# A two-layer graph attention kernel: the preparation steps split into bank fills and bank readers, and the last pair's rows kept in SBUF

## The chip, the core and the metric

The kernel runs on one core of a Trainium2 chip, in one launch. The metric is device time in microseconds, from the start to the end of one execution; lower is better. Engines are named as the profile names them: PE (TensorE), PEld (its weight loads), ACT (ScalarE), DVE (VectorE), POOL (GpSimd) and SP (SyncE, which issues the DMAs here).

## The reference, cut to what matters

A graph of N = 4096 nodes with D = 256 features and a 4096 x 4096 adjacency matrix passes through two graph attention layers (H = 8 heads of O = 32), and then through a transformer block masked by the same adjacency. The change touches the graph layers only:

```python
Wh  = jnp.einsum('nd,hdo->hno', x, W)
src = jnp.einsum('hno,ho->hn', Wh, a[:, :O])
dst = jnp.einsum('hno,ho->hn', Wh, a[:, O:])
e = jax.nn.leaky_relu(src[:, :, None] + dst[:, None, :], 0.2)
e = jnp.where(adj[None, :, :] > 0, e, NEG_INF)
out = jnp.einsum('hnm,hmo->hno', softmax(e), Wh)      # one layer, twice:
h = elu(layer(x, W1, a1)) + x;  out = elu(layer(h, W2, a2)) + h
```

## The kernel before, in words

The softmax is never formed. The exponential of a leaky ReLU is one of two products of a term of the row and a term of the column, and which of the two holds depends on the sign of src + dst. So a layer is a sum over neighbours m of values scaled by column terms, once over all neighbours and once over those with a positive sum. The sign becomes a matrix of eight-bit weights (the comparison), the adjacency masks it, and PE multiplies.

**Groups.** The stage runs 256 groups, one after the other: 2 layers l, 4 blocks nb of 8 row tiles, 4 pairs p of heads, 8 groups g of G = 4 column tiles. A group is 8 tiles x 4 column tiles, 32 units of three matmuls (line 1401), with six PSUM banks `bank0` to `bank5` that stay open over the eight groups of a pair. Each group uses 64 weights of `t` (two per unit), so that group i begins at the matmul on `t` number 64 i of the timeline. Groups are numbered 0 to 255 here; layer 1 begins at 128.

**Side work.** What ACT, DVE and POOL do for other groups, and some PE work, is issued between the tiles of a group. Each step has a place between 0 and 1 in the list `side`; after tile n the steps whose place lies in it are issued, so PE, ACT and DVE each get a fixed order written out by hand. The side work of group i is:

- the comparison for group i+2 (`compare`, lines 1100 and 1102): four steps of two 128x1024 comparisons, one on ACT and one on DVE (in some steps both on ACT), and the mask on DVE (line 1115). It writes `t8`, which has three buffers;
- in layer 0 the clipping of adjacency rows (`mask_clip`, line 867, DVE) and their turning (`mask_turn`, four PE transposes of line 890 and an ACT copy, line 892): four units per group in groups 0 to 5, about one later;
- after a pair, its end on DVE and ACT (`pair_end`, lines 1143 to 1186), a few steps per group;
- in groups 0 to 5 (layer 0) and in 122 to 127, 131 and 132 (layer 1) the preparation of four node tiles.

**Preparation.** `preparation(l, q, ...)` takes rows q of the layer's input (`g_rows`, four tiles of 128 x 256). Two steps `features` transpose one half of the columns each into a PSUM bank (PE, line 981) and copy it to `g_ft` (ACT, line 984). Four steps `values(t)` multiply (PE, line 994) and read the bank: a copy of the terms and three exponentials on ACT (lines 1001, 1007, 1008), then a reduction and a product on DVE (lines 1009, 1020, and 1026 from SBUF). Steps `split(t)` cut the product into two halves (ACT line 1032 or DVE line 1034, then POOL line 1035). `term_rows` transposes the row terms (PE line 1040), copies them (ACT line 1044) and stores them. `turn_bank` gives these steps and the turning of masks a bank each, out of two in turn (`turn`, bufs=2): a fill waits until all readers of the bank of two fills ago are done. In layer 1 the product has two buffers (`g_prod`).

**Rows between the layers.** The end of a pair of layer 0 adds the residual into a tile `e_x` and stores 64 columns of a block of 8 tiles to DRAM (`step_out`, lines 1185 and 1186). Layer 1 loads its rows from there (`rows_ahead`, line 743). The last two preparations, q = 6 and 7, need the columns of the last pair of the last block, whose end runs in groups 128 and 129. They are loaded in groups 130 and 131.

## Time and profile before

| | us |
|---|---|
| median of 3 runs (lowest to highest) | 3252.28 (3251.95 to 3252.8) |
| the profiled execution | 3250.22 |
| its span, from the first to the last instruction | 3248.4 |
| PE, PEld, DVE, ACT, POOL busy in it | 3099.1, 2717.4, 2804.6, 2703.1, 1177.5 |
| the graph layers' groups in it | 40.3 to about 1652 |

Busy shares over the whole span mix stages with different limits. The graph layers take half of it, and there PE, ACT and DVE are all nearly always busy in a plain group. So the preparation groups have to be read by themselves, with windows that begin and end at group starts.

### The profile page before, as it was taken

What the parts mean: (1) busy time and instruction counts of PE and PEld (TensorE: products, weight loads), DVE (VectorE), ACT (ScalarE), POOL (GpSimd) and SP (SyncE); (2) the same over time, 40 slices, a digit from 0 to 9 for tenths busy, and PEclk for the clock granted to TensorE, in tenths of its full rate; (3) what the DMA queues carried; (4) which work ended last, traced back from release to release, by engine and by line L of the source; (5) the groups of instructions that cost most, each with busy time, mean ns of one, the idle gap of its engine ahead of it and who ended that gap; (6) DMA issues with size and microseconds to landing.
All of it is one profiled execution on the core that took longest, in us unless ns stands there. A gap on an engine that the chain in (4) does not pass through costs nothing.

```text
span 3248.4 us, 139142 instructions
## 1 busy us (share of the span) xinstructions
PE 3099.1 (95%) x64076; PEld 2717.4 (84%) x64076; DVE 2804.6 (86%) x3102; ACT 2703.1 (83%) x3305; POOL 1177.5 (36%) x536
## 2 busy tenths in 40 slices
PE   5899999999889999999988999999999999997999
PEld 4799999999779999999965888888888888885666
DVE  6899999988889999999966999999999999994121
ACT  5799999999679999999964888888888888884332
POOL 2300000000310000000002998999888998893110
PEclk8999999999999999999999999999999999998999
DMA  7666554420310213120145010101101010004200
GB/s 250 203 198 201 167 185 149 148 74 29 105 42 31 84 54 93 42 75 27 38 121 143 14 40 20 33 27 27 32 24 47 14 40 15 20 7 120 69 33 27
DMA packets 210306, 249.30 MB, mean 77 GB/s; under 512 B 87792, under 2 KB 131056, under 8 KB 209712
## 3 DMA queue, kind: packets, MB, share of 16 engines
q1 hardware_dynamic: 209712, 240.31, 24.1%
q8 instruction: 503, 8.24, 1.1%
q14 instruction: 91, 0.75, 0.1%
HBM read 197.80 MB, written 42.47 MB: 74 GB/s over the span
## 4 chain that ended last, share of the span: by engine, by line
PE 44%; ACT 4%; DVE 3%; DMA 2%; issue 1%; POOL 0%; SPq 0%; POOLq 0%; DVEq 0%; ACTq 0%
PE u_ps L1725 15%; PE u_av L1743 14%; PE u_dn L1743 8%; PE misc L1931 3%; ACT t L1100 2%; PE misc L1668 2%; PE misc L1915 1%; PE misc L1687 1%; DMA u_xres<-rows 1%; DVE t L1102 1%; DVE t L1115 1%; PE misc L1488 1%; ACT ln_square L1455 0%; POOL u_xres L1874 0%; PE misc L1879 0%
## 5 line engine op out<-in xcount | busy, mean ns | idle before, releaser
L1401 PE MATMUL bank<-vst,t 128*128 128x132 f16 x16384 | 1451.0, 220 | 32.0 <-DVE t L1115 31.5
L1816 POOL TENSOR_TENSOR u_both<-u_e 128x1024 f32<-128x1024 f32 x448 | 1052.5, 2391 | 934.0 <-DVE u_e L1734 931.7
L1401 PE MATMUL bank<-vst,mask 128*128 128x66 f16 (+1 forms) x10296 | 1345.3, 206 | 0.0
L1100 ACT ACTIVATE t<-s_b,g_terms 128x1024 int8<-128x1024 f32 x1231 | 1318.9, 1154 | 27.6 <-PE bank L1401 21.7
L1401 PEld LDWEIGHTS <-t 128*128 128x128 fp8e4 x16384 | 1183.5, 97 | 47.1 <-DVE t L1115 36.6
L1734 DVE SCALAR_TENSOR_TENSOR u_e<-u_mask,u_ps 128x1024 f32<-128x1024 uint8 x1024 | 1165.9, 1215 | 10.3 <-ACT u_ps L1732 6.9
L1732 ACT ACTIVATE u_ps<-u_ps 128x1024 f32<-128x1024 f32 x1024 | 1030.1, 1009 | 142.1 <-PE u_ps L1725 44.0
L1401 PEld LDWEIGHTS <-mask 128*128 128x128 fp8e4 x10296 | 903.5, 98 | 0.0
L1115 DVE SCALAR_TENSOR_TENSOR t<-mask,t 128x2048 int32<-128x2048 int32 x256 | 591.3, 2310 | 82.6 <-ACT t L1100 72.4
L1725 PE MATMUL u_ps<-u_q,u_k 128*32 128x512 f16 x8192 | 637.1, 383 | 11.9 <-DVE u_e L1734 11.2
L1743 PE MATMUL u_av<-u_e,u_v 128*32 128x128 f32 x16384 | 601.8, 273 | 0.6 <-issue 0.6
L1743 PEld LDWEIGHTS u_av<-u_e,u_v 128*32 128x32 f32 x16384 | 488.9, 110 | 129.5 <-issue 2.6
L1102 DVE TENSOR_SCALAR t<-s_b,g_terms 128x1024 fp8e4<-128x1024 f32 x817 | 583.8, 747 | 2.6 <-DMA s_b<-s_d 2.6
L1035 POOL TENSOR_TENSOR vst<-g_prod,vst 128x528 f16<-128x528 f32 x36 | 44.2, 1244 | 777.8 <-DVE vst L1034 757.4
L1743 PE MATMUL u_dn<-u_both,u_ones 128*32 128x128 f32 x7168 | 280.2, 273 | 0.0
L1725 PEld LDWEIGHTS <-u_k 128*32 128x32 f16 x8192 | 228.6, 95 | 57.4 <-issue 16.2
L1743 PEld LDWEIGHTS u_dn<-u_both,u_ones 128*32 128x32 f32 x7168 | 212.9, 110 | 41.1 <-issue 0.5
L1922 ACT ACTIVATE u_hid<-misc,n_b 128x512 f32<-128x512 f32 x64 | 42.7, 682 | 149.5 <-PE misc L1915 149.5
L1938 DVE TENSOR_TENSOR u_xres<-u_xres,misc 128x256 f32<-128x256 f32 x32 | 13.5, 421 | 121.1 <-PE misc L1931 121.1
L1931 PE MATMUL misc<-u_w,u_hid 128*128 128x256 f32 x512 | 111.8, 379 | 0.0
L1915 PE MATMUL misc<-ln_cols,u_w 128*128 128x512 f32 x256 | 111.2, 592 | 0.0
L1931 PEld LDWEIGHTS misc<-u_w,u_hid 128*128 128x128 f32 x512 | 96.8, 190 | 13.2 <-issue 0.5
(147 smaller groups left out, 1916.4 us busy)
## 6 DMA issues: line engine op xcount, KB each, us to landing
g_adj<-in_adj_dram SPq DMA_DIRECT2D x123, 512.0 KB
s_b<-s_d SPq DMA_DIRECT2D x64, 512.0 KB
mask<-mask SPq DMA_DIRECT2D x128, 256.0 KB
u_mask<-mask SPq DMA_DIRECT2D x32, 512.0 KB
mask<-stage SPq DMA_DIRECT2D x48, 256.0 KB
rows<-e_x SPq DMA_DIRECT2D x32, 256.0 KB
half_d<-u_halves SPq DMA_DIRECT2D x32, 256.0 KB
u_q<-half_d SPq DMA_DIRECT2D x32, 256.0 KB
```

Source lines behind the costliest of these rows:

```text
L1100: nc.scalar.activation(to.bitcast(I8), s, AF.Sign, bias=negd, scale=-1.0)
L1102: nc.vector.tensor_scalar(to, s, negd, -1.0, op0=ALU.is_ge, op1=ALU.mult, saturate=False)
L1115: nc.vector.scalar_tensor_tensor(both, m32.unsqueeze(1).to_broadcast(list(both.shape)), SIGNS, both, op0=ALU.bitwise_or, op1=ALU.bitwise_and,)
L1401: nc.tensor.matmul(to, left, right, start=k not in opened, stop=last)
L1668: nc.tensor.matmul(pq, wq_sb[k][:, i * D + c * P : i * D + (c + 1) * P], hn[:, k, :], start=(k == 0), stop=(k == DC - 1),)
L1725: nc.tensor.matmul(ps[r * O : (r + 1) * O, j, :], k_st[:, h, at : at + O], q_st[:, h, :], start=True, stop=True,)
L1732: nc.scalar.activation(ps, ps, AF.Exp, scale=SCALE)
L1734: nc.vector.scalar_tensor_tensor(e, mask, 0.0, ps, op0=ALU.not_equal, op1=ALU.mult)
L1743: nc.tensor.matmul(to[j * O : (j + 1) * O, at], lefts[j], es[j // 2][:, j % 2, at], start=first and part == 0, stop=last and part == PARTS ...
L1816: nc.gpsimd.tensor_tensor(both, es_of[i - 1][u], es_of[i][u], op=ALU.add)
L1915: nc.tensor.matmul(ph, w1_sb[:, k, f * P : (f + 1) * P], hn[:, k, :], start=(k == 0), stop=(k == DC - 1),)
L1931: nc.tensor.matmul(po[:, :D], hid[:, f, at : at + P], w2_sb[:, f, :], start=(f == 0), stop=(f == FC - 1),)
```

## The change

**Fill and readers apart.** Each bank's use in `preparation` and `mask_turn` becomes two steps: an "out" step that fills the bank on PE, and an "in" step that reads it. In the groups with preparation the uses stand in one list: two features, then each value behind a turn of a mask as long as there are any, then the term rows. This is eleven uses in layer 0, seven in layer 1. Use k is filled at place (k + 0.5) slots and read at (k + 0.5 + delay) slots; a slot is 0.9 / (number of uses) and delay is 0.3 with turns and 0.6 without. The split of a value comes 1.5 slots after its reading. The comparison's first place moves from 0.25 to 0.3 in these groups. In the value's reading the copy of the terms moves behind the three exponentials.

**Places by unit.** Side steps are issued after each unit of three matmuls, no longer after each tile, except that what is left waits for the end of the last tile.

**Rows inside SBUF.** For the last pair of layer 0's last block the residual sum is written by two DVE additions of four tiles straight into the `g_rows` tiles of q = 6 and 7, and stored from there with two DMAs. The other 192 columns of these tiles are loaded at the start of group 128. The loads in groups 130 and 131 are gone.

```diff
-        def features(c):
+        def features_out(c):
-            pt = bank()
+            pt = held["f", c] = bank()
...
-            nc.scalar.copy(L.ft[q][:, c, :], pt)
-                if (l > 0 or q > 1) and (l == 0 or q + 1 != NG - 2):
+                if (l > 0 or q > 1) and (l == 0 or q + 1 < NG - 2):
                     rows_ahead(l, q + 1)
+        def features_in(c):
+            nc.scalar.copy(L.ft[q][:, c, :], held.pop(("f", c)))
...
-            nc.scalar.copy(
-                L.terms[:, :, at, :], pv[:, D : D + 2 * H].rearrange("p (k h) -> p k h", k=2)
-            )
+        def values_in(t):
+            at = G * q + t
+            pv = held.pop(("v", t))
             big = some.tile([P, 2, H], F32, name="g_big", bufs=4)
             ... three exponentials
+            nc.scalar.copy(
+                L.terms[:, :, at, :], pv[:, D : D + 2 * H].rearrange("p (k h) -> p k h", k=2)
+            )
             nc.vector.tensor_reduce(
...
+        keeps = l + 1 < NL and first + n == NT and p + 1 == H // 2
+        def step_out_and_keep():
+            x, ex = held["x"], held["ex"]
+            for k in range(n // G):
+                to = coming_rows[l + 1, first // G + k][:, :, cols]
+                nc.vector.tensor_tensor(
+                    to.rearrange("p t (j o) -> p t j o", j=2),
+                    x[:, k * G : (k + 1) * G], ex[:, k * G : (k + 1) * G], op=ALU.add,
+                )
+                nc.sync.dma_start(
+                    rows[l + 1].blocks[nb][k * G * P : (k + 1) * G * P, cols].rearrange(
+                        "(t p) d -> p t d", p=P
+                    ),
+                    to,
+                )
...
-        if i + 1 in prepared and prepared[i + 1][0] > 0:
-            if prepared[i + 1][1] in (0, NG - 2):
-                rows_ahead(*prepared[i + 1])
+        if i + 1 in prepared and prepared[i + 1][0] > 0 and prepared[i + 1][1] == 0:
+            rows_ahead(*prepared[i + 1])
+        if l > 0 and (nb, p, g) == (0, 0, 0):
+            for q in (NG - 2, NG - 1):
+                rows_ahead(l, q, D - 2 * O)
+        turning = list(turns.get(i, ()))
         if made:
-            steps = preparation(*made, lambda: turn_bank([P, 512], F32))
+            features, values, splits, term_rows = preparation(
+                *made, lambda: turn_bank([P, 512], F32)
+            )
+            uses = list(features)
+            delay = 0.3 if turning else 0.6
+            for t in range(G):
+                if turning:
+                    u = turning.pop(0)
+                    uses.append((lambda u=u: turn_out(*u), lambda u=u: turn_in(*u)))
+                uses.append(values[t])
+            uses.append(term_rows)
+            slot = 0.9 / len(uses)
+            for k, use in enumerate(uses):
+                side.append(((k + 0.5) * slot, use[0]))
+                side.append(((k + 0.5 + delay) * slot, use[1]))
+                if use in values:
+                    side.append(((k + 2.0 + delay) * slot, splits[values.index(use)]))
-            beside(steps, 0.0, 0.9)
...
-            beside(steps[:-1], 0.25 if made else 0.0, 0.95)
+            beside(steps[:-1], 0.3 if made else 0.0, 0.95)
...
+                while side and side[0][0] * tiles * G < n * G + m + 1 and not (
+                    n == tiles - 1 and m == G - 1
+                ):
+                    side.pop(0)[1]()
...
-            while side and (n == tiles - 1 or side[0][0] * tiles < n + 1):
+            while side and n == tiles - 1:
                 side.pop(0)[1]()
```

More of the change, by code (lines that the diff above doesn't have):

```diff
@@ L878, in mask_clip, with turn_out @@
             load_ahead(1)
-    def mask_turn(nb, c, i):
+    turned = {}
+    def turn_out(nb, c, i):
         if i == 0:
@@ L890, in mask_turn, with turn_in @@
             nc.tensor.transpose(pt[:, m, :], v[:, m * P : (m + 1) * P], ident_h)
+        turned[nb, c, i] = pt
+    def turn_in(nb, c, i):
+        pt = turned.pop((nb, c, i))
         to = built[nb, c][:, i // 2].bitcast(U16)
@@ L897, in mask_turn @@
             )
+    def mask_turn(nb, c, i):
+        turn_out(nb, c, i)
+        turn_in(nb, c, i)
     def mask_fetch(l, nb, c):
@@ L963, in weights_steps, with rows_ahead @@
         return steps + [step_ends]
-    def rows_ahead(l, q):
+    def rows_ahead(l, q, width=D):
         if q < NG:
-            coming_rows[l, q] = rows_p.tile([P, G, D], F32, name="g_rows")
-            rows[l].load(coming_rows[l, q], G * q)
+            r = coming_rows[l, q] = rows_p.tile([P, G, D], F32, name="g_rows")
+            rows[l].load(r[:, :, :width], G * q, slice(0, width))
     def preparation(l, q, bank, first=False):
@@ L983, in features, with values_out @@
                 )
-            nc.scalar.copy(L.ft[q][:, c, :], pt)
             if c == DC - 1:
                 del coming_rows[l, q]
-                if (l > 0 or q > 1) and (l == 0 or q + 1 != NG - 2):
+                if (l > 0 or q > 1) and (l == 0 or q + 1 < NG - 2):
                     rows_ahead(l, q + 1)
-        def values(t):
-            at = G * q + t
-            pv = bank()
+        def features_in(c):
+            nc.scalar.copy(L.ft[q][:, c, :], held.pop(("f", c)))
+        def values_out(t):
+            pv = held["v", t] = bank()
             for c in range(DC):
@@ L1035, in split, with term_rows_out @@
             nc.gpsimd.tensor_tensor(halves[:, :, 1, :], part, halves[:, :, 0, :], op=ALU.subtract)
-        def term_rows():
-            pr = bank()[: G * H, :P]
+        def term_rows_out():
+            pr = held["r"] = bank()[: G * H, :P]
             nc.tensor.transpose(
@@ L1042, in term_rows, with term_rows_in @@
             )
+        def term_rows_in():
             sr = some.tile([G * H, P], F32, name="g_sr", bufs=1)
-            nc.scalar.copy(sr, pr)
+            nc.scalar.copy(sr, held.pop("r"))
             for t in range(G):
@@ L1047, in term_rows @@
                 nc.sync.dma_start(s_d[l][:, at : at + P], sr[t * H : (t + 1) * H])
-        steps = [lambda c=c: features(c) for c in range(DC)]
-        for t in range(G):
-            steps.append(lambda t=t: values(t))
-            if t > 0:
-                steps.append(lambda t=t: split(t - 1))
-        return steps + [term_rows, lambda: split(G - 1)]
+        features = [(lambda c=c: features_out(c), lambda c=c: features_in(c)) for c in range(DC)]
+        values = [(lambda t=t: values_out(t), lambda t=t: values_in(t)) for t in range(G)]
+        splits = [lambda t=t: split(t) for t in range(G)]
+        return features, values, splits, (term_rows_out, term_rows_in)
     def check_values(l):
@@ L1192, in pair_end @@
             [step_load, step_add], [step_scale], [step_subtract], [step_invert, step_divide],
-            [step_exp], [step_below, step_above], [step_out],
+            [step_exp], [step_below, step_above],
+            [step_out_and_keep if keeps else step_out],
         ])
@@ L1269, in turn, with both @@
             mask_turn(*units[k])
-        first, second = (preparation(0, q, spare_bank, True) for q in range(2))
-        for step in first[:DC] + second[:DC]:
-            step()
+        def both(use):
+            use[0]()
+            use[1]()
+        (f_0, v_0, part_0, row_0), (f_1, v_1, part_1, row_1) = (
+            preparation(0, q, spare_bank, True) for q in range(2)
+        )
+        for use in f_0 + f_1:
+            both(use)
         for step in weights_steps(0):
             step()
-        del first[:DC], second[:DC]
-        value = [[steps[k] for k in (0, 1, 3, 5)] for steps in (first, second)]
-        part = [[steps[k] for k in (2, 4, 6, 8)] for steps in (first, second)]
-        row = [steps[7] for steps in (first, second)]
-        for step in value[0][:2]:
-            step()
+        for use in v_0[:2]:
+            both(use)
         for k in range(2):
             clip(k)
-            value[0][2 + k]()
-        row[0]()
+            both(v_0[2 + k])
+        both(row_0)
         for k in range(4):
-            value[1][k]()
-            part[0][k]()
+            both(v_1[k])
+            part_0[k]()
             if k < 2:
@@ L1291, in begin @@
             if k > 1:
-                part[1][k - 2]()
-        row[1]()
+                part_1[k - 2]()
+        both(row_1)
         s_of[0, 0, 0] = s_fetch(0, 0, 0)
@@ L1298, in begin @@
             if k < 2:
-                part[1][2 + k]()
+                part_1[2 + k]()
             clip(4 + k)
@@ L1328, in graph_attention @@
         made = prepared.get(i)
-        if i + 1 in prepared and prepared[i + 1][0] > 0:
-            if prepared[i + 1][1] in (0, NG - 2):
-                rows_ahead(*prepared[i + 1])
-        if made:
-            steps = preparation(*made, lambda: turn_bank([P, 512], F32))
+        if i + 1 in prepared and prepared[i + 1][0] > 0 and prepared[i + 1][1] == 0:
[4 more added lines that the diff above has]
+        turning = list(turns.get(i, ()))
+        if made:
+            features, values, splits, term_rows = preparation(
+                *made, lambda: turn_bank([P, 512], F32)
+            )
+            uses = list(features)
[12 more added lines that the diff above has]
+                    side.append(((k + 2.0 + delay) * slot, splits[values.index(use)]))
             if made[1] == NG - 1:
-                steps.append(lambda: check_values(made[0]))
-            beside(steps, 0.0, 0.9)
+                side.append((0.99, lambda: check_values(made[0])))
         if i + 2 < len(groups):
             steps = compare(i + 2)
-            beside(steps[:-1], 0.25 if made else 0.0, 0.95)
+            beside(steps[:-1], 0.3 if made else 0.0, 0.95)
             beside(steps[-1:], 0.96, 1.0)
@@ L1347, in graph_attention @@
             beside([lambda step=step: step(lambda: turn_bank([P, HB], F32)) for step in mine], 0.0, 0.9)
-        beside([lambda u=u: mask_turn(*u) for u in turns.get(i, ())], 0.0, 0.9)
+        beside([lambda u=u: mask_turn(*u) for u in turning], 0.0, 0.9)
         clips = turns.get(i + 2, ()) if i >= NG - 2 else turns.get(i + 1, ())
```

## The prediction

> **What bounds the kernel now.** I first cut the graph layers at their group starts (windows view), since the page's busy shares average over stages with different limits. Columns: stretch, length, busy time of PE, PEld, DVE, ACT, POOL, clock, DMA.

> ```profile
> 40.30:61.09 20.79, 16.16 (x149) 13.86 (x150) 15.09 (x27) 13.52 (x33) 2.70 (x2) 0.73 0.84 287
> 61.09:137.31 76.22, 61.79 (x749) 52.30 (x747) 61.37 (x111) 54.50 (x151) 30.02 (x21) 1.00 0.61 194
> ...
> 1016.14:1061.66 45.52, 45.07 (x906) 44.95 (x904) 43.07 (x47) 44.35 (x48) 0.00 (x0) 1.00 0.15 41
> ...
> 820.89:831.61 10.72, 10.72 (x137) 9.60 (x135) 8.84 (x16) 7.89 (x25) 2.25 (x2) 1.00 0.33 99
> 831.61:901.36 69.75, 58.81 (x669) 50.34 (x667) 55.12 (x100) 45.23 (x133) 24.39 (x20) 0.95 0.32 101
> 901.36:922.13 20.77, 17.74 (x328) 17.26 (x326) 18.84 (x26) 18.21 (x22) 2.46 (x3) 1.00 0.15 41
> 922.13:952.48 30.35, 24.64 (x267) 21.42 (x267) 19.83 (x36) 17.30 (x51) 7.16 (x6) 0.89 0.16 45
> 952.48:971.34 18.86, 15.84 (x349) 15.60 (x346) 18.53 (x25) 17.00 (x20) 2.60 (x2) 1.00 0.17 59
> ```

> See the third row: eight plain groups take 45.52 us, 5.69 each, with PE busy throughout. Nothing is to be had there. In the preparation groups PE has holes: 19.1 us in groups 0 to 5 (first two rows), none in 122, 10.9 in 123 to 127, 3.0 in 128 to 130, 5.7 in 131 and 132, 3.0 in 133 to 135; 41.8 in all. Then I asked what ends the holes (timelines of PE, ACT and SP, by start, length, idle time before):

> ```profile
> 64.31 0.66 PE L981 MATMUL turn<-ident,g_rows 128*128 128x128 f32 x4 [1.68 <-ACT g_ft L984]
> 69.98 1.16 PE L994 MATMUL turn<-g_w_ext,g_ft 128*128 128x272 f32 x4 [0.58 <-DVE ev_broad L1026]
> 72.77 1.16 PE L994 MATMUL turn<-g_w_ext,g_ft 128*128 128x272 f32 x4 [0.69 <-DVE ev_broad L1026]
> ...
> 849.82 1.89 PE L994 MATMUL turn<-g_w_ext,g_ft 128*128 128x272 f32 x4 [1.87 <-ACT g_ft L984]
> ...
> 926.51 1.97 PE L981 MATMUL turn<-ident,g_rows 128*128 128x128 f32 x8 [3.49 <-DMA g_rows<-rows]
> ```
> ```profile
> 846.57 0.63 ACT L1032 CAST vst<-g_prod 128x528 f16<-128x528 f32 x1 [1.41 <-DVE g_prod L1026]
> 847.11 2.18 ACT L1100 ACTIVATE t<-s_b,g_terms 128x1024 int8<-128x1024 f32 x2
> 849.20 1.05 ACT L984 COPY g_ft<-turn 128x512 f32<-128x512 f32 x2
> ```

> In layer 0 the second feature waits for the bank of the first (1.68), and values wait for each other through DVE (0.58, 0.69). In layer 1 the first value waits for the feature copies: ACT first idled 1.41 us for a split, then did two comparisons. At 926.51 the rows of q = 6 come late: stored at 919.90, asked for at 922.51.

> **The change, part by part.** No work is added: the same PE fills, ACT and DVE readings and POOL halves. Only orders change.

> *Layer 1, groups 123 to 127.* Seven uses take the two banks in turn, so a value has two fills' time for its bank. PE needs (58.81 - 3.15)/5 = 11.1 us a group; the 3.15 are explained below. ACT: the two comparisons of the last step (place 0.869) now come before the last split (0.977), so the 1.41 us hole is filled with work. Walked from the last value's fill, at T: ACT reads it to T + 0.6, compares to 2.7, copies the term rows to 2.95, splits to 3.6, copies the features to 4.7. PE meanwhile ends the group (9 units x 0.178 + 0.2 = 1.8), does 11 units and two features of the next (2.0 + 1.0) and is at the first value at T + 4.8. The copy just makes it: the hole of 1.87 closes. DVE is busy 55.12/5 = 11.0 a group. The mask's wait for ACT (1.2 to 1.8 us before) goes. What stays is the wait of the third or fourth product for POOL with two `g_prod` buffers, 7.8 us over the eight groups, about 1.0 each; the spacing of split and value stays near half a slot to one. So DVE sets 11.0 + 1.0, and 0.2 for what rubs: 12.2. Five groups: 61.0 instead of 69.75, -8.75. Group 122, without holes: +0.2 for the later first value.

> *Layer 0.* Eleven uses alternate turns and values, which puts all four values of a group on the same bank. One cycle is fill 1.0, ACT 0.45, DVE reduction, product and small product 1.1, latencies 0.2: 2.8 us (before: fill ends 68.35, 71.14, 73.93, so 2.79). Three cycles: 8.4 us, where PE has only 7.0 us of work (16 units x 0.178, three turns of 0.38, three values of 1.0). From the fourth fill to the next group's first value: ACT reads, compares 2.1, copies term rows, splits, copies the first feature by T + 3.95, where PE wants its bank at T + 3.65; the value ends at T + 5.75. A group takes 14.15 us against 76.22/5 = 15.24: five groups, -5.5. The 1.68 goes, part of it comes back as a third wait between values. Group 0 (20.79 us, at clock 0.73) loses some of its 2.8 us hole: -2, between 0 and -5, as the DMA share of 0.84 lets it gain little.

> *Rows in SBUF.* The wait of 3.49 us goes, with the half clock around it. Cost: one 128x512 addition becomes two of 128x256 on DVE (0.69 together, plus some 0.1), two stores, and two loads issued in group 128 ahead of the residual's load on SP (0.9 us of issue, nobody waits). Stores land beside other work; their next reader is layer 1's fourth block. Moved past SP's queue, the loads stand behind the earlier pair's store and the freeing of the two `g_rows` buffers by group 127's transposes, both before 901, and ahead of nothing urgent. New waits: the additions wait for these loads, issued some 15 us earlier; from store to first use a load takes 4 us here (922.51 to 926.51), so 0. If they were late, DVE's next mask would stand behind them, and PE behind that; then the gain shrinks towards 0. The transposes now wait for the additions, which end near 919.9, and start near 922.5: it fits by 2.6 us. Group 131 then starts as 122 did, with ACT still comparing for 2 us: 11.3 instead of 17.1. Group 132: 12.2 instead of 13.25. Together -6.85.

> *Groups 128 to 130 and 133 to 135.* DVE is the late one there (18.84 of 20.77, 18.53 of 18.86). It enters each stretch late by its wait for ACT, 1.8 us both times, which goes; but little other slack: -1.5 and -1.0.

> *Finer places and the terms' copy.* In plain groups the order on ACT and DVE is unchanged; PE's turns come up to 0.5 us earlier, and their clips stand a group ahead: 0. Moving the copy is worth 0 if DVE starts behind ACT's last reading, -0.1 a value if not. DVE's reduction starts 0.03 us after the last exponential (67.14 after 67.11), so 0.

> [...]

> ```profile
> 850.20:853.50 3.30, 3.30 (x18) 2.66 (x17) 3.21 (x4) 0.44 (x5) 0.04 (x1) 0.50 0.86 257
> ...
> 891.20:894.50 3.30, 3.06 (x14) 2.41 (x15) 2.63 (x3) 1.45 (x7) 0.06 (x1) 0.50 0.77 229
> ...
> 925.30:932.00 6.70, 5.49 (x32) 4.78 (x33) 1.15 (x1) 1.36 (x5) 0.00 (x0) 0.50 0.52 149
> ```

> Three stretches run at half clock; the first two follow holes of only 1.87 us. [...] By the rows they go with the holes. I take the rows, since in 820 to 971 us no half clock stands without a hole right before it.

> **Sum.** -8.75 + 0.2 - 5.5 - 2 - 6.85 - 1.5 - 1.0 = -25.4. The profiled execution, 3250.22 us, becomes 3224.8. The median stands 2.06 above it: 3226.9, rounded 3227.

> **Rivals.** *PE-bound (0.15).* The values' chain in layer 0 is hidden and DVE in layer 1 keeps up. PE's own work in groups 1 to 5 is 61.79/5 = 12.4 each. Then groups 0 to 5 take 5 x 12.4 + 16.2 = 78.2 (-18.8), 122 to 127 take 10.7 + 55.5 (-14.3), 131 and 132 22 (-8.3), and the two other stretches lose 6: -47, 3205. For it: DVE needs 12.3 in layer 0. Against: the 2.79 us between fills were measured with DVE waiting for ACT, not short of time.

> *The holes only move (0.09).* The values' cycle on one bank reaches 3.1 us as clips (0.69) and comparisons (0.75) stand ahead of reductions, so layer 0 gains nothing, and POOL waits grow to 2.5 us a group in layer 1. Only the row wait stays gained: about -6, 3246. For it: DVE waited for POOL 1.02 us at 858.25. Against: ACT's idle 1.41 plainly leaves.

> *Slower (0.06).* In the eighth group of each pair, steps placed by unit go ahead of the copies that free the six banks (line 1407). At 1152.75 the copy of bank 4 ends 1.82 us before PE reopens it at 1154.57; banks 1 and 2 have 3.6. The places put one comparison (1.05 us) ahead of banks 1 and 2 and none ahead of bank 4, so I expect no wait. If three came ahead of bank 4, 3.15 - 1.82 = 1.33 us at 31 pair ends is +41: 3268. It decides from 1.82 + 25.4/31 = 2.6 us of work moved ahead.

> **How the numbers follow.** The main case (0.70) alone gives 3217 to 3237: a group of layer 0 between 13.2 and 14.8, of layer 1 between 11.4 and 13. The range 3208 to 3242 reaches into the PE-bound case and most of the way to the third. What this kernel can tell from no change is about 0.2%, 6.5 us. Faster: 0.70 + 0.15 + 0.02 of the third; same: 0.07; slower: 0.06.

> **Right or wrong.** Right: no wait of line 981 for a DMA near 900 us; no hole of line 994 behind `g_ft` over 0.5 us; no half clock between 820 and 970; groups 123 to 127 near 12.2 us, groups 1 to 5 near 14.2 with line 994 waiting for DVE three times each. Wrong: groups 1 to 5 under 13 or over 15, DVE waiting for POOL over 15 us in layer 1's preparation, or PE waiting for line 1407 at pair ends.

## The result, and the profile after

| | before | after |
|---|---|---|
| median of 6 runs, us | 3252.11 (3246.91 to 3252.8) | 3235.02 (3231.98 to 3237.0) |
| ratio, 95% interval | 1 | 0.9949 [0.9936, 0.9962] |
| profiled execution, its span | 3250.22, 3248.4 | 3235.03, 3232.9 |

The change saves 17.1 us, where 25.4 were forecast. (A hole, below, is a stretch in which PE idles.) Line numbers of the kernel after are higher: the features' transposes are line 991 (before 981), their copies 1000, the values 1005 (994), the terms' copy 1020 (1001), DVE's reduction, product and small product 1023, 1034 and 1040, the split 1046 to 1049, the term rows 1054 and 1060, the clip 867 and the comparison 1114 and 1116, the mask 1129 (1115), the units 1452 (1401).

The windows view of the kernel after, cut at group starts as before. The rows are group 0, groups 1 to 5, 122, 123 to 127, 128 to 130, 131 and 132, 133 to 135; columns as before (length, PE, PEld, DVE, ACT, POOL, clock, DMA):

```profile
39.89:59.08 19.19, 15.34 (x149) 13.18 (x150) 15.29 (x27) 14.48 (x32) 3.52 (x3) 0.84 0.89 280
59.08:130.50 71.42, 61.68 (x750) 53.07 (x748) 62.83 (x111) 55.99 (x150) 31.17 (x21) 1.00 0.69 215
813.16:825.19 12.03, 10.76 (x137) 9.58 (x135) 9.96 (x18) 8.70 (x26) 2.25 (x2) 1.00 0.30 89
825.19:888.33 63.14, 55.30 (x669) 48.14 (x667) 56.39 (x98) 45.16 (x134) 34.14 (x20) 1.00 0.41 124
888.33:909.20 20.87, 18.84 (x328) 18.71 (x326) 20.73 (x28) 17.56 (x21) 4.60 (x2) 0.92 0.22 53
909.20:932.53 23.33, 21.73 (x271) 19.21 (x269) 19.27 (x34) 17.88 (x51) 9.10 (x6) 1.00 0.01 2
932.53:953.87 21.34, 17.43 (x349) 17.18 (x346) 20.04 (x25) 16.31 (x20) 4.06 (x2) 0.92 0.16 52
```

See the fourth row. PE now idles 63.14 - 55.30 = 7.8 us in these five groups where it idled 10.9. DVE's busy time has gone up from 55.1 to 56.4 us and POOL's from 24.4 to 34.1, although neither was given any more work. In the fifth row DVE has no slack at all. Against before: group 0 -1.6 us, groups 1 to 5 -4.8, 122 +1.3, 123 to 127 -6.6, 128 to 130 +0.1, 131 and 132 -7.0, 133 to 135 +2.5; the start and groups 6 to 121 -1.3. That is -17.5; what comes behind group 135 took 1.9 us more in this profile, which makes the 15.5 us between the two spans.

What ends PE's holes now (timeline of PE, kernel after):

```profile
79.67 1.15 PE L1005 MATMUL turn<-g_w_ext,g_ft 128*128 128x272 f32 x4 [0.74 <-DVE ev_broad L1040]
82.45 1.16 PE L1005 MATMUL turn<-g_w_ext,g_ft 128*128 128x272 f32 x4 [0.50 <-ACT t L1114]
85.22 1.16 PE L1005 MATMUL turn<-g_w_ext,g_ft 128*128 128x272 f32 x4 [0.51 <-ACT t L1114]
...
849.37 0.27 PE L1054 MATMUL turn<-ident,g_terms 128*32 128x128 f32 x1 [0.97 <-DVE g_prod L1034]
```

In layer 0 each group has the three waits of a value for a value that the prediction named, 2.78 us apart. (The profile puts the second and third down to a comparison on ACT, but that one ends 0.01 us after PE's weight load for the value has begun. In all three the load begins 0.03 us after DVE's last instruction of the value before, line 1040: it is the bank, read last by DVE.) In layer 1 the feature copies are no longer waited for. What is new is the last row: the transpose of the term rows waits for a bank that DVE is late in reading. And DVE is late for this reason (timelines of DVE and POOL, same kernel):

```profile
839.94 2.28 DVE L1129 SCALAR_TENSOR_TENSOR t<-mask,t 128x2048 int32<-128x2048 int32 x1
842.14 1.63 DVE L1116 TENSOR_SCALAR t<-s_b,g_terms 128x1024 fp8e4<-128x1024 f32 x1
...
848.53 0.69 DVE L1034 TENSOR_TENSOR g_prod<-turn,g_big 128x512 f32<-128x512 f32 x1 [1.38 <-POOL vst L1049]
```
```profile
840.19 4.59 POOL L1049 TENSOR_TENSOR vst<-g_prod,vst 128x528 f16<-128x528 f32 x2 [2.81 <-DVE vst L1048]
847.35 2.25 POOL L1049 TENSOR_TENSOR vst<-g_prod,vst 128x528 f16<-128x528 f32 x2 [2.57 <-DVE g_tops L1023]
```

POOL's two subtractions take 2.25 us by themselves and 4.59 beside the mask (3.04 for the first of them, where one alone takes 1.15), and the comparison behind the mask takes 1.63 us instead of 0.74. That is one cost: two engines hold each other up. The other is the 1.38 us in which a product waits for its buffer, which POOL has still to read.

### The profile page after: what moved, and what is told of

Read it like the earlier page. It is cut to its first block, busy times and chain, and to the rows that moved or that the text cites. A ratio compares the mean times of both kernels' runs of the same rounds, so it can differ in the third digit from the quotient of the medians.

```text
span 3232.9 us, 139161 instructions
## 1 busy us (share of the span) xinstructions
PE 3094.6 (96%) x64076; PEld 2713.6 (84%) x64076; DVE 2812.3 (87%) x3103; ACT 2702.9 (84%) x3305; POOL 1193.7 (37%) x536
## 4 chain that ended last, share of the span: by engine, by line
PE 44%; ACT 3%; DVE 3%; DMA 2%; issue 1%; POOL 0%; SPq 0%; POOLq 0%; DVEq 0%; ACTq 0%
PE u_ps L1780 15%; PE u_av L1798 14%; PE u_dn L1798 8%; PE misc L1986 3%; ACT t L1114 2%; PE misc L1723 2%; PE misc L1742 1%; PE misc L1970 1%; DMA u_xres<-rows 1%; DVE t L1116 1%; DVE t L1129 1%; PE misc L1543 1%; POOL u_xres L1929 0%; ACT ln_square L1510 0%; DMA out_dram<-u_xres 0%
## 5 line engine op out<-in xcount | busy, mean ns | idle before, releaser
L1789 DVE SCALAR_TENSOR_TENSOR u_e<-u_mask,u_ps 128x1024 f32<-128x1024 uint8 x1024 | 1166.0, 1214 | 10.8 <-ACT u_ps L1787 7.5
L1049 POOL TENSOR_TENSOR vst<-g_prod,vst 128x528 f16<-128x528 f32 x36 | 59.5, 1668 | 749.5 <-DVE vst L1048 736.9
L1986 PEld LDWEIGHTS misc<-u_w,u_hid 128*128 128x128 f32 x512 | 96.7, 190 | 13.3 <-issue 0.5
```

What stands on the lines that cost most here:

```text
L1789: nc.vector.scalar_tensor_tensor(e, mask, 0.0, ps, op0=ALU.not_equal, op1=ALU.mult)
L1986: nc.tensor.matmul(po[:, :D], hid[:, f, at : at + P], w2_sb[:, f, :], start=(f == 0), stop=(f == FC - 1),)
```

## The experiments

Times by stage, from the group starts in each profile, in us. A stretch of 3.4 us at half clock in a stage is marked *, two of them **. Group 0, which starts at half clock in every profile, is not marked.

| kernel | 0 | 1-5 | 122 | 123-127 | 128-130 | 131 | 132 | 133-135 |
|---|---|---|---|---|---|---|---|---|
| before | 20.8 | 76.2 | 10.7 | 69.8** | 20.8 | 17.1** | 13.3 | 18.9 |
| after | 19.2 | 71.4 | 12.0 | 63.1 | 20.9* | 11.4 | 11.9 | 21.3* |
| e1 rows alone | 20.7 | 76.3 | 10.7 | 69.7** | 20.8 | 10.9 | 14.7* | 19.4* |
| e2 no rows | 18.5 | 71.5 | 12.0 | 63.2 | 19.4 | 18.1** | 11.9 | 21.3* |
| e3 more products | 19.7 | 71.4 | 10.9 | 65.4* | 18.6 | 10.7 | 10.8 | 20.6* |
| e4 no POOL | 20.1 | 71.5 | 10.9 | 57.3 | 17.2 | 10.8 | 10.8 | 17.2 |
| e5 pairs | 18.6 | 77.0* | 12.0 | 63.1 | 19.5 | 11.4 | 12.0 | 19.8 |
| e6 terms first | 18.8 | 70.9 | 12.0 | 62.8 | 19.7 | 11.4 | 12.0 | 21.3* |
| e7 finer places | 20.2 | 74.9 | 10.9 | 66.7 | 20.1 | 16.3* | 12.7 | 19.2* |
| e8 splits ahead | 19.8 | 71.4 | 11.1 | 62.4 | 19.0 | 10.9 | 11.8 | 21.3* |
| e9 last split later | 19.7 | 71.4 | 11.1 | 59.8 | 18.9 | 10.9 | 11.4 | 21.0* |
| e10 order in layer 0 | 19.2 | 70.7 | 12.0 | 63.2 | 19.5 | 11.4 | 12.0 | 19.8 |
| e11 e9 and e10 | 19.8 | 70.7 | 11.1 | 59.8 | 18.9 | 10.9 | 11.4 | 22.0** |
| e12 e11 and relief | 19.2 | 70.7 | 11.1 | 60.8 | 17.9 | 10.9 | 11.4 | 20.2* |

The ratios below are to the kernel before on the same chip. Against the kernel after, the runs are compared by these ratios (0.9949 for the kernel after).

**e1, the row part alone** (on the kernel before):

```diff
-            if prepared[i + 1][1] in (0, NG - 2):
+            if prepared[i + 1][1] == 0:
                 rows_ahead(*prepared[i + 1])
+        if l > 0 and (nb, p, g) == (0, 0, 0):
+            for q in (NG - 2, NG - 1):
+                rows_ahead(l, q, D - 2 * O)
...
-            [step_exp], [step_below, step_above], [step_out],
+            [step_exp], [step_below, step_above],
+            [step_out_and_keep if keeps else step_out],
```

> The kernel before with one part of the change: the last pair's rows stay in SBUF, everything else as before. Theory A (the row part is worth its wait and the half clock around it): group 131 falls from 17.1 to about 11.5-12 us, the rest of the groups stays, total about -5.5 us against before. Rival (DVE's backlog takes it back): the wait for the rows had given DVE time to catch up; without it groups 132 to 135 lose 2-4 us, and the total is -2 to -3 us.

Measured: 3246.03 us, 3249.92 before; ratio 0.9986 [0.9979, 0.9993], -3.9 us. Group 131 falls by 6.2 us. Group 132 gains 1.4 and 133 to 135 gain 0.5, both with a half-clock stretch that the kernel before does not have there. Theory A holds for the wait; part of it goes to a half clock behind the next hole, not to DVE's backlog.

**e2, the row part undone** (on the kernel after; e1's lines the other way round).

> The changed kernel with the row part undone (rows of q = 6 and 7 stored, then loaded in groups 130 and 131). Theory A: group 131 goes from 11.4 to about 17 us, total +5.5 us against the changed kernel. Rival (backlog): 131 loses 5.5 us, but 133 to 135, 21.3 us in the changed kernel, go back to about 18.9, so that the total is only +3 us.

Measured: 3238.61 us; ratio 0.9970 [0.9958, 0.9981]. Group 131 goes to 18.1 us, 6.7 more than after. 133 to 135 stay at 21.3, so the wait for the rows had not covered them: the rival falls.

**e3, products in other buffers** (on the kernel after):

```diff
+            elif l > 0 and t > 1:
+                wide = rows_p.tile([P, 2, G * P], I32, name="g_adj", bufs=3)
+                prod = held[t] = (
+                    wide.rearrange("p a b -> p (a b)").bitcast(F32)[:, : H * 2 * V1]
+                    .rearrange("p (h i v) -> p h i v", h=H, i=2)
+                )
```

> The changed kernel, in which the products of the third and fourth value in layer 1 lie in buffers that are idle at that time, so that no product waits for POOL to have read the one of two values before. Theory A (in layer 1's preparation DVE is the bound: 11.3 us busy and 1.35 us idle, mostly for POOL): groups 123 to 127 fall from 12.6 to about 11.6 us, 122 from 12.0 to about 11, total -6 to -8 us. Rival B (the two PSUM banks in turn are the bound, the POOL wait lies beside it): no group changes by more than 0.3 us, total within 2 us.

Measured: 3231.14 us; ratio 0.9944 [0.9928, 0.9961]. Group 122 falls by 1.1 us and 131 and 132 by 1.8 together, as theory A has it. But 123 to 127 do not fall, even without the half-clock stretch there, and in all only 1.6 us are gained by the ratios where 6 to 8 were forecast. The wait for the buffer is gone, but DVE is busy 61.0 us instead of 56.4. Five more instructions fall into the stretch; the rest are longer ones: from 814 to 905 us the comparison's mean goes from 933 to 1043 ns and the mask's from 2377 to 2514, and a comparison beside POOL at 849.40 takes 1.71 us. Much of what was a wait has become longer instructions.

**e4, no POOL in layer 1** (on the kernel after):

```diff
+            if l == 0:
                 nc.gpsimd.tensor_tensor(halves[:, :, 1, :], part, halves[:, :, 0, :], op=ALU.subtract)
```

> The changed kernel without POOL's subtraction in layer 1 (the lower halves of the split values are left out there). It takes away the wait for POOL and also what POOL's instructions do to DVE's when both run. [...] Rival B (banks): within 2 us.

Measured: 3217.45 us; ratio 0.9901 [0.9885, 0.9918]. All of layer 1's stages fall, 16.5 us in all against after, which is more than the 11 to 13 that I had expected if POOL's instructions lengthen DVE's (6 to 8 if only the wait for POOL counts): 128 to 135 lose 9.6 us, not 2 to 3, of which some 3 are the half-clock stretches of the kernel after. The windows view (groups 123 to 127) and the groups of lines on DVE (814 to 905 us, in which e4 gets further, so that it has more comparisons), first after, then e4:

```profile
825.48:882.80 57.32, 54.81 (x669) 48.00 (x667) 49.34 (x101) 45.06 (x134) 0.00 (x0) 1.00 0.45 136
```
```profile
L1116 DVE TENSOR_SCALAR t<-s_b,g_terms 128x1024 fp8e4<-128x1024 f32 x26 | 24.2, 933 | 0.0
L1034 DVE TENSOR_TENSOR g_prod<-turn,g_big 128x512 f32<-128x512 f32 x24 | 16.3, 680 | 6.1 <-POOL vst L1049 6.1
```
```profile
L1119 DVE TENSOR_SCALAR t<-s_b,g_terms 128x1024 fp8e4<-128x1024 f32 x31 | 22.8, 744 | 0.0
L1034 DVE TENSOR_TENSOR g_prod<-turn,g_big 128x512 f32<-128x512 f32 x24 | 16.3, 680 | 0.0
```

DVE's busy time falls from 56.4 to 49.3 us by taking away work of POOL alone; the comparison's mean goes from 933 to 744 ns, while the product, which reads PSUM, keeps its 680. So POOL cost DVE 1.4 us of busy time a group and 1.0 to 1.4 of waiting. With both gone PE is nearly the bound, 54.8 of 57.3. So it is shown that POOL's subtractions lengthen DVE's instructions, and by how much; in what way they do it no run shows.

**e5, pairs of values** (on the kernel after, layer 0): the uses in the order turn, value, value, turn, turn, value, value, turn.

```diff
+                uses += [wave[0], values[0], values[1], wave[1]]
+                uses += [wave[2], values[2], values[3], wave[3]]
```

> The changed kernel with another order of the uses in layer 0: turn, value, value, turn, turn, value, value, turn, so that neighbouring values take different banks and a bank's next fill is a turn. Theory A (the changed kernel keeps all four values of a group on one bank, three cycles of 2.78 us): groups 1 to 5 fall from 14.3 to 12.6-13.3 us, group 0 by about 1, total -6 to -9 us against the changed kernel. Rival (DVE, 12.6 us busy a group there, is the bound as in layer 1): groups 1 to 5 stay above 13.9, total within 2 us.

Measured: 3241.43 us; ratio 0.9986 [0.9977, 0.9995]: groups 1 to 5 rise to 77.0 us, one half-clock stretch included. Neither theory. By the ratios this is 12 us slower than the kernel after; the profile, of the second fastest of the 12 runs (3237.4 to 3249.0 us), shows 5.6 of them in groups 1 to 5. Over the 12 runs the time goes with the mean granted clock (0.987 to 0.990 up to 3244.0 us, 0.984 to 0.986 from 3246.2 us on), as more half-clock stretches would give; where they lie is not on record. The timelines of PE and ACT:

```profile
62.21 0.66 PE L991 MATMUL turn<-ident,g_rows 128*128 128x128 f32 x4 [1.94 <-ACT g_sr L1060]
```
```profile
59.83 2.19 ACT L1114 ACTIVATE t<-s_b,g_terms 128x1024 int8<-128x1024 f32 x2
61.92 0.24 ACT L1060 COPY g_sr<-turn 32x128 f32<-32x128 f32 x1
```

With a turn as the last fill before the term rows, the next group's first feature finds its bank held by readers that stand on ACT behind the two comparisons of the last step. The values' waits have shrunk to about 0.5, and 1.94 us of waiting stands elsewhere.

**e6, the terms' copy first again** (on the kernel after):

```diff
+            nc.scalar.copy(
+                L.terms[:, :, at, :], pv[:, D : D + 2 * H].rearrange("p (k h) -> p k h", k=2)
+            )
             big = some.tile([P, 2, H], F32, name="g_big", bufs=4)
```

> The changed kernel with the copy of the terms back in front of the three exponentials. Theory A (DVE's reduction starts behind ACT's last reading of the bank, whichever that is): no group changes by more than 0.1 us, total within 2 us. Rival (the product gets its factors 0.07 us earlier per value with the exponentials first): layer 0's groups, bound by the values' cycle, get 0.2-0.3 us longer each, total +2 us.

Measured: 3230.1 us; ratio 0.9948 [0.9931, 0.9964], the ratio of the kernel after. Groups 1 to 5 are 0.5 us shorter in all, 0.1 each, so the rival points the wrong way. The copy's place is worth 0 in the time.

**e7, finer places alone** (on the kernel before):

```diff
+                while side and side[0][0] * tiles * G < n * G + m + 1 and not (
+                    n == tiles - 1 and m == G - 1
+                ):
+                    side.pop(0)[1]()
-            while side and (n == tiles - 1 or side[0][0] * tiles < n + 1):
+            while side and n == tiles - 1:
```

> The kernel before with only the places by unit instead of by tile, its preparation steps still fill and read in one. Theory A (the finer places alone are worth nothing, since PE's fills and ACT's and DVE's orders stay): plain groups 6 to 121 and 136 to 255 within 1 us in all, preparation groups within 0.3 us each, total within 2 us of before. Rival (the fills come up to 0.5 us earlier to PE and this is a part of the gain): groups 1 to 5 and 123 to 127 fall by 0.5 us each, total -5 us.

Measured: 3244.75 us, 3247.81 before; ratio 0.9990 [0.9983, 0.9997], -3.1 us. Plain groups moved by 1.0 us in all. Groups 1 to 5 fell by 1.3 us: the wait at the second feature is 1.32 instead of 1.68. Groups 123 to 127 fell by 3.1 us, which is about what the two half-clock stretches cost that this profile does not have there, with holes of 1.0 to 2.1 us still in place. The interval, -1.0 to -5.5 us, leaves out 0 and lies between the two theories.

**e8, splits ahead of the next value** (on the kernel after, layer 1):

```diff
-            if first or t % 2 == 1:
+            if first or (t % 2 == 1 and l == 0):
...
-                    side.append(((k + 2.0 + delay) * slot, splits[values.index(use)]))
+                    behind = 2.0 if wave else 1.0
+                    side.append(((k + behind + delay) * slot, splits[values.index(use)]))
```

> The changed kernel with, in layer 1 alone, all four splits' first halves on DVE and each split half a slot ahead of the next value's reading instead of behind it, so that POOL's subtraction runs beside DVE's reduction and product (which read PSUM) instead of beside the mask and the comparisons, and is done before its product buffer is wanted. [...] Rival (what costs is DVE's amount of work): groups 123 to 127 rise by 0.7 us each, total +4 us.

Measured: 3228.65 us; ratio 0.9941 [0.9924, 0.9957]. By the ratios 2.6 us are gained where I had expected 6 to 9. 122 and 128 to 132 fall by 3.5 us (some 1.4 of it is the half-clock stretch of group 130), 123 to 127 by only 0.7. The buffer wait is gone and DVE no longer idles; but POOL's last subtraction still meets the mask, and takes 3.04 us.

**e9, the last split in the next group** (on e8):

```diff
+                    elif t < G - 1:
+                        side.append(((k + 1.0 + delay) * slot, splits[t]))
+                    else:
+                        carried.append(splits[t])
...
+        while carried:
+            side.append((0.395 if made else 0.3, carried.pop()))
```

> The kernel of the splits ahead of the next value (layer 1), in which the last split of a group moves from just ahead of the mask into the next group, just ahead of that group's first value. [...] Rival (DVE's amount of work is the bound): no change.

Measured: 3224.65 us; ratio 0.9925 [0.9908, 0.9941], 4.0 us below e8. Groups 123 to 127 are 59.8 us. The timelines of DVE and POOL in e9:

```profile
837.88 2.28 DVE L1129 SCALAR_TENSOR_TENSOR t<-mask,t 128x2048 int32<-128x2048 int32 x1
840.08 0.74 DVE L1116 TENSOR_SCALAR t<-s_b,g_terms 128x1024 fp8e4<-128x1024 f32 x1
...
842.01 0.50 DVE L1040 TENSOR_SCALAR g_prod<-g_big 128x16 f32<-128x16 f32 x1
```
```profile
836.49 1.45 POOL L1049 TENSOR_TENSOR vst<-g_prod,vst 128x528 f16<-128x528 f32 x1 [1.20 <-DVE vst L1048]
841.33 1.15 POOL L1049 TENSOR_TENSOR vst<-g_prod,vst 128x528 f16<-128x528 f32 x1 [3.40 <-DVE vst L1048]
```

The comparison behind the mask is back at 0.74 us, with the same instructions in another order. What is left of the collision is the small product of line 1040, 0.50 us here instead of 0.17. DVE is busy 57.9 of 59.8 us, so it binds; but not all of this is work. The small product takes 459 ns in the mean, 171 in e4, so that 21 of them still lose about 6 us to POOL. The groups come at 12.0 us, just above the 11.4 to 11.8 that I had expected.

**e10, another order in layer 0** (on the kernel after):

```diff
+                uses += [wave[0], values[0], values[1], wave[1]]
+                uses += [wave[2], values[2], wave[3], values[3]]
```

> The changed kernel with the order turn, value, value, turn, turn, value, turn, value of the uses in layer 0: the values take both banks, but the last fills before the term rows stay as in the changed kernel, so that no feature waits for a turn behind the two comparisons of the last step. Theory A (one value behind a value on the same bank instead of three): PE's holes fall from 1.95 to about 1.2 us a group, groups 1 to 5 from 14.3 to 13.3-13.8 us, total -3 to -5 us. Rival (DVE and ACT set the pace of the values in any order): groups 1 to 5 within 0.3 us of 14.3.

Measured: 3233.5 us; ratio 0.9946 [0.9927, 0.9964]; groups 1 to 5 fall by 0.7 us in all, 0.14 each. Two values behind each other still wait 0.7 us, and turns now wait 0.5 us for a turn that ACT reads behind a comparison. The rival holds: with two banks the waits change place.

**e11, e9 and e10 together.**

> Both of the two last edits on the changed kernel. If they act in different stages they add: total -9 to -15 us against the changed kernel, and groups 1 to 5 and 123 to 127 as in the two kernels alone. Rival (what layer 1's groups gain is given back in 128 to 135, where DVE is late): 133 to 135 stay at 21 us or more, and the total is -5 to -8 us.

Measured: 3224.9 us; ratio 0.9925 [0.9909, 0.9942]. Each stage is that of the kernel with the edit, except that 133 to 135 have two half-clock stretches. They stay at 22.0 and the total is 7.8 us below the kernel after, as the rival has it; but without the half clock 133 to 135 would be near 19 us (an estimate from PE's busy time in the two stretches), so the rival's number there is the clock's doing.

**e12, three comparisons on ACT** (on e11):

```diff
+        if l > 0 and (nb, p) == (0, 0):
+            more += (6, 10, 29)
```

> The kernel with both edits (splits ahead and last split deferred, new order in layer 0), in which three comparisons of layer 1's first pair (column tiles 6, 10 and 29) move from DVE to ACT, which idles 3 us in groups 128 to 130 and 4 us in 133 to 135. Theory A (what stays of the loss in 128 to 135 is DVE entering these groups late with no slack): the first matmul's waits for the mask shrink by 0.7 us each, 128 to 130 fall from 18.9 to 17.5-18.4, 133 to 135 from 22.0 (with a half-clock stretch) or about 20 (without) by 0.7, total -1 to -3 us. Rival (the masks there wait for ACT): no gain, or +1 us.

Measured: 3226.92 us; ratio 0.9938 [0.9922, 0.9955]. The stages go as theory A has them, 128 to 130 by -1.0 and 133 to 135 by -1.8 us (with one half-clock stretch less), but 123 to 127 lose 1.0, where one of the three falls; the time shows no gain. e9 and e11 are the fastest versions that compute everything, about 24 us below before, 7 more than the change.

## Why the prediction was right, and where it was off

**Right.** The time lies in the range, on the side forecast, by the main case. Groups 1 to 5 came at 14.28 us each (forecast 14.15), with the chain on one bank at 2.78 us a cycle (2.8). That the chain alone sets this pace is not shown: e10 has one of these waits in a group instead of three and gains only 0.14 us a group, and DVE is busy 62.8 of the 71.4 us. Groups 131 and 132 came at 23.3 us (23.5): the wait of 3.49 us and the half clock around it left, and e1 and e2 show it for group 131 (-6.2, +6.7). The holes behind the feature copies closed. The copy's place was worth 0 (e6), and nothing waits for line 1407's copies at pair ends.

**DVE in 123 to 127: the term "11.0 + 1.0 + 0.2".** It came to 12.63 us a group, 11.28 busy and 1.35 idle. I took DVE's busy time of before, 11.0, as its work. e4 shows that its work is 49.34/5 = 9.9 us, and that the rest was already time held up by POOL. A row of the kernel before shows it, and I did not use it:

```profile
849.33 3.06 DVE L1115 SCALAR_TENSOR_TENSOR t<-mask,t 128x2048 int32<-128x2048 int32 x1 [1.20 <-ACT t L1100]
```

POOL's subtraction of 849.10 ran until 850.24, and the mask took 3.06 us instead of 2.28. The mask's wait for ACT, which I counted as a gain, had kept most of POOL's work ahead of the mask; without it the mask begins first (839.94, POOL 840.19 in the rows above), and POOL and the comparison behind the mask pay. In both rows what began first kept its time (the subtraction 1.14 us, the mask 2.28), and the other took longer. POOL's subtraction that starts 0.25 us into the mask ends 1.0 us behind it, where one alone takes 1.15 us: by my estimate from these times only some 0.15 us of it was done beside the mask. The product that reads PSUM meets nothing (680 ns with POOL and without; 0.68 us at 841.42 in e9, beside the subtraction of 841.33).

PE's 11.1 us a group, (58.81 - 3.15)/5 in the prediction, did not bind. The 3.15 us were an estimate, about half of PE's busy time in the two stretches at half clock (3.30 and 3.06 us). e4, at full clock throughout, shows 54.81 us of PE, 11.0 a group.

**Group 122: "+0.2".** It came to +1.3. The product's wait for its buffer reaches PE: the bank of the third value is also that of the term rows, so 1.3 us of DVE waiting became a hole at line 1054. e3, e8 and e9 take it away (10.9 to 11.1).

**128 to 130 and 133 to 135: "-1.5 and -1.0".** They came to +0.1 and +2.5. e10, which has the kernel after's code there, has 19.5 and 19.8 us without a half-clock stretch: so -1.3 and +0.9 by the orders, and 1.4 and 1.6 by the clock. The first is nearly the forecast: the mask's wait for ACT left, and with it the hole of group 128. What is left there, a hole of 2.0 us in group 129, is POOL's: e4 does not have it.

In 133 to 135, e10 against before, group 133 has -0.4, 134 has +1.3 and 135 has 0. The wait for ACT left here too. But POOL's last subtractions now meet DVE's masks: at 933.72 and 937.05 two small masks and a large one take 3.30 and 3.12 us in the kernel after, 3.09 and 2.29 before, 2.35 and 2.29 in e4. The 1.3 us of group 134 come from a part of the edit that the sum does not have. Six small checks on DVE, which end the preparation of a layer, moved from ahead of a mask to behind it (before, then after):

```profile
955.05 0.15 DVE L709 TENSOR_SCALAR checks<-check_top 128x1 f32<-128x1 f32 x1
958.25 2.29 DVE L1115 SCALAR_TENSOR_TENSOR t<-mask,t 128x2048 int32<-128x2048 int32 x1
...
963.29 2.29 DVE L1115 SCALAR_TENSOR_TENSOR t<-mask,t 128x2048 int32<-128x2048 int32 x1
```
```profile
937.05 3.12 DVE L1129 SCALAR_TENSOR_TENSOR t<-mask,t 128x2048 int32<-128x2048 int32 x1
940.10 0.17 DVE L705 TENSOR_REDUCE check_top<-g_tops 128x1 f32<-128x32 f32 x1
...
944.23 2.29 DVE L1129 SCALAR_TENSOR_TENSOR t<-mask,t 128x2048 int32<-128x2048 int32 x1
```

From the end of one mask to the end of the next it was 5.0 us and is 6.3, and group 134, which begins and ends behind these masks, is as long. e4 has the same 6.3, and keeps a hole of 1.6 us in group 134 without any work of POOL. No run moved the checks back.

```profile
943.85:947.27 3.42, 1.35 (x33) 1.23 (x30) 3.33 (x4) 1.15 (x1) 0.00 (x0) 1.00 0.59 188
947.27:950.68 3.41, 3.41 (x39) 3.41 (x37) 3.31 (x3) 1.85 (x4) 0.00 (x0) 0.50 0.35 124
```
```profile
939.58:942.99 3.41, 2.21 (x69) 2.08 (x65) 3.32 (x4) 2.50 (x3) 0.00 (x0) 1.00 0.11 43
942.99:946.41 3.42, 2.55 (x47) 2.56 (x48) 3.32 (x5) 0.95 (x3) 0.00 (x0) 1.00 0.84 268
946.41:949.82 3.41, 3.41 (x69) 3.41 (x67) 3.41 (x4) 3.41 (x6) 0.00 (x0) 1.00 0.00 0
```

So a hole of 2 us does not bring the half clock by itself, as I took it from the rows: by these counts it depends on where the hole falls on the grid. The forecast that no half clock would stay between 820 and 970 us failed, and that those of 124 and 127 left is in part luck. By the stages above a half-clock stretch costs about 1.5 us (1.4 and 1.6).

**Finer places: "0".** e7 shows 1.3 us in groups 1 to 5 and 0.6 in 132.

## What to carry to other kernels

When waits are removed from an in-order stage, ask for each remaining engine how much of its busy time is work: leave out the engine that may hold it up, and see whether its instructions get shorter (in e4 the comparison went from 933 to 744 ns). In this kernel the place for POOL's subtractions is beside the product, which reads PSUM (680 ns with POOL and without), and not beside the mask (3.06 us instead of 2.28), the comparison (933 ns in the mean, 744 without POOL) and even the small product (0.50 us in e9 instead of 0.17), which read SBUF alone and were held up. When steps are put into a new list, place every one of them, the small checks too. With two buffers in rotation, an order of fills must be judged with every reader's queue in view; a better order for one use (e5) can put the next one behind the longest instruction of another engine.

## What was not expected of the hardware

A wait and a collision can be the same cost in two guises: with more product buffers (e3) DVE's idle time went, and the comparison's mean rose from 933 to 1043 ns. And a POOL subtraction of 1.15 us that starts 0.25 us into a mask of 2.28 us takes 3.04 us and then holds DVE's next instruction up by 0.9 us; with the split moved by one place (e9) both are gone, while the small product loses more than before. By the counts above, the clock goes with how busy PE was within one window of a grid, and not with the length of a hole. Why 6 of the 14 windows with 1.49 to 1.65 us kept the full clock was not settled.
